# Expert weights, token rows and value tiles asked for in another order in a Trainium2 decoder kernel

## The chip, the core and the metric

One core of a Trainium2 chip runs the whole kernel in one launch. Its engines are PE (matrix products), DVE and POOL (elementwise work), ACT (activation functions and copies out of PSUM) and SP (used here to ask for DMA transfers); they run side by side and wait for each other through semaphores. All transfers between the chip's DRAM and SBUF are DMAs. The metric is the device time of one execution in microseconds (us). All data is fp32.

## What is computed

A decoder of two layers runs on x (4 sequences of 512 tokens, 256 wide) with a context `ctx` (4 x 1601 x 256). Every step is followed by a residual sum and a layernorm:

```python
x = ln(x + ttt(x))               # per token one SGD step on W, b, then W@q + b
x = ln(x + cross(x, ctx))        # one head of 256, a 512x1601 side bias
x = ln(x + experts(x))           # 8 experts, each token goes to 2 of them
x = ln(x + causal_self(x))       # 16 heads of 16
x = ln(x + cross_rope(x, ctx))   # 16 heads of 16, rotary positions, mask
x = ln(x + ffn(x))               # 256 -> 1024 -> 256, dequantized weights, SiLU

def expert(xf, e):
    h = gelu(xf @ Wi[e] + bi[e]) * sigmoid(xf @ Wg[e] + bg[e])   # 256 -> 1024
    r = xf + (h @ Wo[e] + bo[e])                                 # 1024 -> 256
    return (r - mean(r)) * rsqrt(var(r) + eps) * gamma[e] + beta[e]
```

The router takes the softmax of `x @ Wr + br`, keeps the two largest experts of each token and weights their outputs by these two probabilities, scaled to the sum 1.

## The kernel before, in words

**Order.** Nearly all of the program stands in sections of `tc.manual_schedule()`: each engine gets its instructions in the order in which the Python code issues them. Nothing is reordered by a planner around the change, so what stands in front of what on an engine or on a DMA queue is decided by the order of the calls. Tiles come from pools with a fixed number of buffers for each name (`bufs`); a tile that is asked for while all its buffers are taken makes its first writer, often a DMA, wait until the oldest one has been read.

**Stages, in us from the start of the profiled execution.** TTT runs to about 270, the first cross attention to 529, the experts from 529.34 to 1008.62; then attention (causal self attention and cross attention with rope, in units of one sequence and some heads) and the last FFN run to 2423.5.

**End of the first cross attention.** The loop over `steps` (a step is 128 tokens of one sequence) scores, transposes and sums up the weighted context rows. What follows for a sequence, the closing layernorm, the transposes of x, the router and the scatter of its rows into per-expert row lists `xs`, is a generator, `closing(b)`, of which `tail()` runs one more piece. For the last sequence no further steps are there to run beside it. The rope attention's values of contexts 2 and 3 (13 tiles of 128 context rows each, 26 calls of `value(b, k)`) are put there: one 128x256 product into a PSUM tile from `bank()`, and a copy by ACT into a row of 16 heads with a column of ones each. `rows_of_values` prepares those rows by DVE memsets. The tuple `(0, 4, 0, 0, 0, 12, ...)` says how many values follow each piece of the tail; the ten left over come after `blocks_left()`, which computes on the chip which rows and weights the pair blocks below need (`xrow`, `wrow`, and a count). The finished rows go to DRAM as `vd[2]` and `vd[3]`.

**Experts.** A block is 256 token rows. A block of kind "f" (first) is the first 256 rows of an expert: weights and rows come through SP's queue from known places. A block of kind "m" (more) is a pair of 128-row halves, which may belong to two different experts: rows are asked for by POOL with an indirect DMA per half (`rows_of`, index `xrow`), and so are the weights (`load_expert`, index `wrow`), for each half its own `eWi`, `eWg` and `eWo`. An `eWo` tile of 1408 KB also holds the bias, the scale (gamma) and the shift (beta). The order is "ffmfmfmmfmfmmfmfmmm", 19 blocks. For each block `i`, `run` calls

- `first_half`: 2 x 64 products with eWi into gelu and with eWg into sigmoid, the product `g` by DVE; as soon as a weight tile has been read, the next block's is asked for (`eWi`, `eWg` have two buffers in `pmw`);
- `turned` of the next block: four transposes of its rows `xb` by PE, copied to `xbT` by DVE;
- `second_half` of the block before: 2 x 16 products with eWo, the residual sum (L991) and bias by DVE, moments and the square root, the layernorm (L999), then scale and shift and the store to `ys`.

The end of `second_half` is what the change touches. For each half it reads in the kernel before

```python
eng = nc.gpsimd if nxt else nc.vector
eng.tensor_tensor(r[:, hs], r[:, hs], gam, ALU.mult)
eng.tensor_tensor(r[:, hs], r[:, hs], bet, ALU.add)
... # the store of r to ys
for half in range(2) if len(wos) == 1 else (h,):
    if nxt:
        weights_of(nxt, "eWo", half)
```

and after both halves `rows_of(after)`. `nxt` is the block after the one that this second half belongs to, `after` the one two further on. `eWo`, `rb` (the tile of `r`), `g` and `xbT` have two buffers in `p3`, `xb` has three. Between the blocks `next(work)` runs one piece of `attention_first`, small preparations of the attention stage.

**Start of attention.** When the count says that no expert has rows left over, `rest` (a branch) is skipped and attention begins. The two expert outputs of each token are gathered by POOL and summed; x is normalized and transposed. The first keys and values do not depend on x: `keys0` are the rope keys of context 0, two calls of `key` (one for each half of the features) for each of the four chunks of 512, 512, 512 and 65 context rows. `key` makes a product, lets ACT write it with its bias to a `raw` tile (four buffers), calls `rotated` (a DVE shuffle, then two products with the cosine and sine tables and a sum by the engine `eng`, L1281 to L1284) and stores it to `kcd` in DRAM, from where it is read back head by head. `key`'s engine is chosen as `nc.gpsimd if here is None or i % 2 else nc.vector`, inside a lambda that reads `eng` when it runs; the loop's last `i` is 3, so that every key of context 0 runs on POOL. `values_tile` makes the tile of values `v0` with two memsets. The order of the first calls is written out by hand:

```python
for f in keys0[0:2] + values1[:8] + add + values1[8:] + turn + keys0[4:6]:
    f()
for f in (k0_, q0_, rows0, *self_values(0), *keys0[2:4], *keys0[6:8]):
    f()
```

`add` sums the expert outputs into x (L1221), `turn` transposes it, `k0_` and `q0_` are keys and queries of the self attention, `rows0` reads them back in the layout for heads. L1401 is the first DVE operation of the attention units on scores (it adds the causal bias and finds the row maximum).

Of the kernel before, what the change touches and what calls it, by code (L numbers as in the profile page):

```python
# [9 lines left out]
F32 = mybir.dt.float32  # L10
# [3 lines left out]
ALU = mybir.AluOpType  # L14
# [3 lines left out]
P = 128  # L18
# [21 lines left out]
def decoder(ctx: ExitStack, tc: tile.TileContext, a: dict, out: bass.AP):  # L40
# [358 lines left out]
    def load_expert(e, names, pool):  # L399

        ts = []
        for name in names:
            t = pool.tile([P, a[name].shape[1]], F32, tag=name, name=name)
            if isinstance(e, int):
                nc.sync.dma_start(t, a[name][e * P : (e + 1) * P, :])
            else:
                nc.gpsimd.indirect_dma_start(
                    t, None, a[name], bass.IndirectOffsetOnAxis(ap=e, axis=0)
                )
            ts.append(t)  # L410
        return ts
# [214 lines left out]
    with tc.tile_pool(name="p2", bufs=2) as p2, ExitStack() as ordered:  # L626
# [138 lines left out]
        values, places = [], {}  # L765

        def rows_of_values():
            big = p2in.tile([P, NT * S2], F32, tag="fs", name="v23")
            rest = p2in.tile([P, KHALF * D], F32, tag="ctxa", name="v2")
            for i in range(NKT):  # L770
                places[3, i] = big[:, i * VROW : (i + 1) * VROW]
                j = NKT + i
                places[2, i] = (
                    big[:, j * VROW : (j + 1) * VROW] if i < 9 else rest[:, (i - 9) * VROW : (i - 8) * VROW]
                )
            for b_ in (2, 3):
                nc.vector.memset(places[b_, NKT - 1], 0.0)
            for t in (big[:, : 22 * VROW], rest[:, : 4 * VROW]):
                t = t.rearrange("p (k r) -> p k r", r=VROW)
                nc.vector.memset(t[:, :, NH * VW :], 0.0)  # L780
                heads = t[:, :, : NH * VW].rearrange("p k (h r) -> p k h r", r=VW)
                nc.vector.memset(heads[:, :, :, HD : HD + 1], 1.0)

        def value(b, k):
            kn = kn_of(k)
            ps = bank()[:, :D]
            mm(ps[:kn], [(ctxTs[b][:, c, k * P : k * P + kn], xaV[:, c, :]) for c in range(2)])
            dst = places[b, k][:kn, : NH * VW].rearrange("p (h r) -> p h r", r=VW)
            nc.scalar.copy(dst[:, :, :HD], ps[:kn].rearrange("p (h r) -> p h r", r=HD))
            if b == 2 and k == NKT - 1:  # L790
                nc.sync.dma_start(vd[2][:, : 9 * VROW], big_of(2, 0, 9))
                nc.sync.dma_start(vd[2][:, 9 * VROW :], big_of(2, 9, NKT))
            if b == 3 and k == NKT - 1:
                nc.sync.dma_start(vd[3], big_of(3, 0, NKT))
# [9 lines left out]
        for i in range(len(steps) + 1):  # L804
# [8 lines left out]
            if i < len(steps):  # L813
                turned(*steps[i])
            tail()
# [8 lines left out]
        values = [lambda b=b, k=k: value(b, k) for b in (2, 3) for k in range(NKT)]  # L824


        for n in (0, 4, 0, 0, 0, 12, 0, 0, 0, 0, 0):
            if n == 4:
                tail()
                rows_of_values()  # L830
            else:
                tail()
            for f in values[:n]:
                f()
            values = values[n:]
# [44 lines left out]
    def values_tile(pool, name, n):  # L880
        t = pool.tile([P, n, NH * VW + HD - 1], F32, tag=name, name=name)
        nc.gpsimd.memset(t[:, :, NH * VW :], 0.0)
        heads = t[:, :, : NH * VW].rearrange("p k (h r) -> p k h r", r=VW)
        nc.gpsimd.memset(heads[:, :, :, HD : HD + 1], 1.0)
        return t


    with tc.tile_pool(name="p3", bufs=2) as p3, ExitStack() as ordered:
# [87 lines left out]
        def second_half(block, nxt, after):  # L976
# [6 lines left out]
            for h in range(2):  # L983
# [19 lines left out]
                eng = nc.gpsimd if nxt else nc.vector  # L1003
                eng.tensor_tensor(r[:, hs], r[:, hs], gam, ALU.mult)
                eng.tensor_tensor(r[:, hs], r[:, hs], bet, ALU.add)
# [4 lines left out]
                for half in range(2) if len(wos) == 1 else (h,):  # L1010
                    if nxt:
                        weights_of(nxt, "eWo", half)
            if after:
                rows_of(after)

        def attention_first():
# [40 lines left out]
            ready["vals"] = [values_tile(p4a, "v0", NKT)]  # L1057
# [50 lines left out]
        def run(blocks, work):  # L1108
# [4 lines left out]
            for name in ("eWi", "eWg", "eWo"):  # L1113
                for h in range(2):
                    if (blocks[0], name) not in first_loads:
                        weights_of(blocks[0], name, h)
            turned(blocks[0])
            for i, b in enumerate(blocks):
# [3 lines left out]
                if i:  # L1122
                    second_half(blocks[i - 1], b, get(i + 2))
# [3 lines left out]
            second_half(blocks[-1], None, None)  # L1127
# [30 lines left out]
    with ExitStack() as s4:  # L1158
# [17 lines left out]
        def one():  # L1176
            return spare() if alone else ps1.tile([P, 512], F32, tag="one", name="one")

        diagq, later_, qt, kself, ngs, vself, vals = (
            ready[k] for k in ("diagq", "later", "qt", "ks", "ngs", "vself", "vals")  # L1180
        )
        kcross = group_tiles(p4c, "kc", S2)
# [122 lines left out]
        def context(b, keys, values, here=None):  # L1305
# [20 lines left out]
            for i in sorted({*keys, *values}):  # L1326
# [5 lines left out]
                eng = nc.gpsimd if here is None or i % 2 else nc.vector  # L1332
# [406 lines left out]
        for f in (k0_, q0_, rows0, *self_values(0), *keys0[2:4], *keys0[6:8]):  # L1739
            f()  # L1740
# [246 lines left out]
```

## Time and profile before

| | us |
|---|---|
| three executions | 2431.46, 2424.82, 2430.93 |
| their median | 2430.93 |
| the profiled execution, its own time | 2425.35 |
| its span (first to last instruction) | 2423.5 |
| PE busy | 2289.2 (94%) |
| DVE busy | 1197.9 (49%) |
| ACT busy | 1063.4 (44%) |
| POOL busy | 435.3 (18%) |
| expert stage, first eWi to last eWo product | 479.28, PE busy 432.99 |
| attention and FFN, 1104 to the end | 1319.6, PE busy 1300.7 |

The page of the profile first gives busy times, then forty slices of 60.6 us with the busy share of each engine in tenths. PEclk in the slices is the clock that the throttle granted to PE, in tenths of full speed. "L202" is line 202 of the kernel's program; nearly all products go through one helper, so they are told apart by their tiles (`bank<-eWo,g`). In an answer on waits a row reads: the engine and tile that waited, what ended the wait, the sum of us, how many waits, the longest. In a timeline a row reads: start, duration, engine, line, operation, output and inputs, the number of instructions, and in brackets the idle time before it and what ended that.

### The profile page before, as it was taken

The page shows a single profiled execution, that of the slowest core. Times are in us where ns is not written, and L with a number is a line of the kernel's source. Part 1 is how long each engine was busy: PE and PEld are TensorE (multiplying, and loading weights), DVE is VectorE, ACT ScalarE, POOL GpSimd, SP SyncE. Part 2 cuts the span into 40 slices and gives each one's busy share as a digit, 9 for nine tenths or more (in the row PEclk, how much of TensorE's full clock was granted, in tenths as well). Part 3 has the DMA queues.
Part 4 walks back from the last instruction along what each step waited for, and adds up shares of the span by engine and source line. Part 5 has one row for each costly group of instructions (what it writes and reads, how often), then busy time and mean ns, then how long its engine had stood idle before and what let it go on. Part 6 is the DMA issues. An engine that isn't in the chain of part 4 may idle for free.

```text
span 2423.5 us, 36202 instructions
## 1 busy us (share of the span) xinstructions
PE 2289.2 (94%) x14448; PEld 1296.1 (53%) x14448; DVE 1197.9 (49%) x2846; ACT 1063.4 (44%) x2103; POOL 435.3 (18%) x455
## 2 busy tenths in 40 slices
PE   7898999979898999789999999999999999999998
PEld 4767677768787888643333334333333333333266
DVE  2343334422232332226666667666766776677334
ACT  1211222124445454234555553655665666556730
POOL 1010001121333334274330010120122010000000
PEclk9999999989999999888999998999999999999999
DMA  8300211145788767432210220111120010100100
GB/s 328 145 1 22 110 55 45 52 165 207 288 327 313 276 264 291 145 115 70 79 44 27 72 72 1 32 38 46 52 73 28 25 59 15 58 6 18 31 9 27
DMA packets 77099, 244.13 MB, mean 101 GB/s; under 512 B 11640, under 2 KB 34686, under 8 KB 64638
## 3 DMA queue, kind: packets, MB, share of 16 engines
q1 hardware_dynamic: 60126, 137.41, 16.7%
q0 software_dynamic: 13632, 89.32, 9.7%
q10 hardware_dynamic: 3168, 15.03, 1.7%
q8 instruction: 116, 1.90, 0.3%
q14 instruction: 57, 0.47, 0.1%
HBM read 196.12 MB, written 56.77 MB: 104 GB/s over the span
## 4 chain that ended last, share of the span: by engine, by line
PE 50%; DVE 1%; ACT 1%; issue 0%; DVEq 0%; ACTq 0%
PE s L1442 23%; PE po L1469 12%; PE one L202 11%; PE s L202 2%; PE s L1452 1%; PE one L1427 1%; PE one L1490 1%; ACT x L171 0%; ACT ex L1456 0%; DVE pm L1399 0%; DVE one L1401 0%; PE one L1511 0%; PE one L1609 0%; PE one L1532 0%; DVE nb L166 0%
## 5 line engine op out<-in xcount | busy, mean ns | idle before, releaser
L1456 ACT ACTIVATE ex<-s 128x512 f32<-128x512 f32 (+1 forms) x1062 | 578.2, 594 | 460.7 <-PE s L1442 225.6
L1399 DVE TENSOR_REDUCE pm<-one 128x1 f32<-128x512 f32 x768 | 493.1, 685 | 162.7 <-PE s L1442 106.9
L1442 PE MATMUL s<-q,kc 32*128 32x512 f32 x1612 | 529.9, 640 | 0.9 <-ACT ex L1456 0.8
L202 PE MATMUL one<-kc,qt 32*128 32x512 f32 (+1 forms) x2048 | 484.4, 564 | 0.3 <-DVE pm L1399 0.3
L1442 PEld LDWEIGHTS s<-q,kc 32*128 32x128 f32 x1612 | 166.3, 179 | 204.1 <-issue 170.4
L1469 PE MATMUL po<-ex,v 128*32 128x256 f32 (+3 forms) x2688 | 252.2, 444 | 0.3 <-ACT ot L1482 0.3
L1401 DVE CUSTOM_DVE_ANT_0 one<-one,c_diagq 128x512 f32<-128x512 f32 x256 | 171.9, 716 | 74.3 <-PE one L202 62.3
L1469 PEld LDWEIGHTS po<-ex,v 128*32 128x32 f32 (+1 forms) x2688 | 54.2, 108 | 253.1 <-issue 246.4
L1442 PE MATMUL s<-q,ks 32*128 32x512 f32 x512 | 180.0, 651 | 5.4 <-ACT ex L1456 4.9
L202 PEld LDWEIGHTS one<-kc,qt 32*128 32x128 f32 x2048 | 164.6, 189 | 11.8 <-DVE pm L1399 7.5
L202 PE MATMUL bank<-eWo,g 128*128 128x256 f32 x608 | 151.9, 410 | 17.1 <-DMA eWo<-in_eWo,wrow 11.3
L202 PE MATMUL one<-ks,qt 32*128 32x512 f32 x512 | 152.6, 665 | 2.2 <-ACT raw L1314 2.2
L1282 POOL TENSOR_TENSOR raw<-raw,c_cos 128x512 f32<-128x512 f32 (+1 forms) x32 | 35.0, 1094 | 629.9 <-DVE swp L1281 570.5
L202 PEld LDWEIGHTS bank<-eWo,g 128*128 128x128 f32 x608 | 123.7, 208 | 40.4 <-issue 10.7
L971 DVE TENSOR_TENSOR g<-g,sg 128x1024 f32<-128x1024 f32 x38 | 46.5, 1224 | 196.4 <-ACT sg L969 177.1
L202 PE MATMUL wide<-xbT,eWi 128*128 128x128 f32 (+1 forms) x960 | 139.5, 306 | 4.0 <-DVE xbT L937 4.0
L202 PEld LDWEIGHTS wide<-xbT,eWi 128*128 128x128 f32 x960 | 130.5, 193 | 12.3 <-issue 3.4
L202 PE MATMUL wide<-xbT,eWg 128*128 128x128 f32 (+1 forms) x960 | 137.0, 303 | 0.0
L202 PEld LDWEIGHTS wide<-xbT,eWg 128*128 128x128 f32 x960 | 128.1, 191 | 6.6
L1442 PEld LDWEIGHTS s<-q,ks 32*128 32x128 f32 x512 | 53.9, 185 | 83.5 <-issue 62.3
L98 ACT ACTIVATE sd<-mv,eps 128x1 f32<-128x1 f32 (+2 forms) x34 | 10.0, 295 | 188.9 <-DVE mv L109 188.8
L202 PE MATMUL wide<-ctxT,q 128*128 128x512 f32 (+1 forms) x256 | 91.3, 510 | 0.8 <-DVE q L667 0.8
(325 smaller groups left out, 3038.2 us busy)
## 6 DMA issues: line engine op xcount, KB each, us to landing
xs<-zero SPq DMA_DIRECT2D x32, 512.0 KB
kc<-kcd SPq DMA_DIRECT2D x16, 800.5 KB
eWo<-in_eWo SPq DMA_DIRECT2D x8, 1408.0 KB
eWi<-in_eWi SPq DMA_DIRECT2D x8, 1028.0 KB
eWg<-in_eWg SPq DMA_DIRECT2D x8, 1028.0 KB
qt<-qd SPq DMA_DIRECT2D x32, 256.0 KB
ctxT<-in_ctxT SPq DMA_DIRECT2D x4, 1601.0 KB
kcd<-in_c_rowkc ACTq DMA_DIRECT2D x4, 1601.0 KB
```

The costliest lines, as they stand in the source:

```text
L98: nc.scalar.activation(sd, mv[:, :, 1], AF.Sqrt, bias=eps)
L202: nc.tensor.matmul(ps, l, r, start=(i == 0), stop=(i == n - 1))
L971: nc.vector.tensor_tensor(part, part, dst, ALU.mult)
L1282: eng.tensor_tensor(raw[:, :n], raw[:, :n], cos[:, :n], ALU.mult)
L1399: nc.vector.tensor_reduce(pm[:, t, j, c : c + 1], ps, AX.X, ALU.max)
L1401: nc.vector.tensor_tensor_reduce(out=ps, in0=ps, in1=diagq[:, 384 - t * P : 896 - t * P], scale=1.0, scalar=LOWEST, op0=ALU.add, op1=ALU.m ...
L1427: nc.tensor.transpose(pt[:, t * P : (t + 1) * P], ng.rearrange("p j r -> p (j r)"), ident)
L1442: nc.tensor.matmul(ps[:kn], kt[rows, k * P : k * P + kn], q2[rows, :], start=True, stop=cross)
L1452: nc.tensor.matmul(ps[:, k * P : (k + 1) * P], later_[:, :P], later_[:, P:], start=False, stop=True)
L1456: nc.scalar.activation(ex[:kn, h, :], ps[:kn], AF.Exp)
L1469: nc.tensor.matmul(state["po"][j * 32 : j * 32 + 32, q0:q1], (vals if cross else vself)[b % 2][:kn, k, c0 : c0 + 32], ex[:kn, j % 2, q0:q1 ...
L1490: nc.tensor.transpose(pt[:, t * P : (t + 1) * P], ot[:, t * P : (t + 1) * P], ident)
```

## The change

It has four parts.

1. In the expert stage `eWo` gets three buffers in place of two. `second_half` asks for the rows of the block two further on first, and for output weights after that, through a new helper `outs`, which keeps a list of all halves of all blocks in order and asks for the next ones whenever fewer than three are taken.
2. Scale and shift of each expert output go to DVE, for all blocks; before, this was so for the last block alone.
3. At the end of the first cross attention the values of contexts 2 and 3 are computed in another order, two to a double PSUM tile from `wide()`, and spread differently over the pieces of the tail; the rows that hold them are prepared in two parts, the large one inside the loop over `steps`.
4. At the start of attention all rotations of context 0's keys go to DVE, the self values come after the keys, and `v0` has a pool of its own on the other side of SBUF, with its memsets on DVE.

The core of the diff (the lines before and after are in the functions printed above; "..." stands for lines left out):

```diff
@@ load_expert
-            t = pool.tile([P, a[name].shape[1]], F32, tag=name, name=name)
+            t = pool.tile(
+                [P, a[name].shape[1]], F32, tag=name, name=name, bufs=3 if name == "eWo" else 2
+            )
@@ end of the first cross attention
-        def rows_of_values():
...
+        def rows_of_values(first):
+
+            name, tag, n = ("v23", "fs", 22) if first else ("v2", "ctxa", 4)
+            t = p2in.tile([P, NT * S2 if first else KHALF * D], F32, tag=tag, name=name)
+            for i in range(n):
+                at = (3, i) if first and i < NKT else (2, i - NKT) if first else (2, 9 + i)
+                places[at] = t[:, i * VROW : (i + 1) * VROW]
+            nc.vector.memset(places[3 if first else 2, NKT - 1], 0.0)
...
         def value(b, k):
             kn = kn_of(k)
-            ps = bank()[:, :D]
+            if not halves or len(halves) == 2:
+                halves[:] = [wide()]
+            else:
+                halves.append(halves[0])
+            ps = halves[0][:, len(halves) - 1, :D]
...
-            if b == 2 and k == NKT - 1:
+            if (b, k) == (2, 8):
                 nc.sync.dma_start(vd[2][:, : 9 * VROW], big_of(2, 0, 9))
+            if (b, k) == (3, NKT - 1):
+                nc.sync.dma_start(vd[3], big_of(3, 0, NKT))
+            if (b, k) == (2, NKT - 1):
                 nc.sync.dma_start(vd[2][:, 9 * VROW :], big_of(2, 9, NKT))
-            if b == 3 and k == NKT - 1:
-                nc.sync.dma_start(vd[3], big_of(3, 0, NKT))
...
             if i < len(steps):
                 turned(*steps[i])
+            else:
+                rows_of_values(True)
...
-        values = [lambda b=b, k=k: value(b, k) for b in (2, 3) for k in range(NKT)]
-
-
-        for n in (0, 4, 0, 0, 0, 12, 0, 0, 0, 0, 0):
-            if n == 4:
+        order = [(2, k) for k in range(9)] + [(3, k) for k in range(NKT)]
+        order += [(2, k) for k in range(9, NKT)]
+        values = [lambda b=b, k=k: value(b, k) for b, k in order]
+        for n in (3, 0, 0, 0, 0, 0, 6, 0, 0, 0, 0, 0):
+            if len(values) < len(order):
                 tail()
-                rows_of_values()
-            else:
-                tail()
+            if len(values) == len(order) - 3 and len(places) == 22:
+                rows_of_values(False)
@@ second_half
-        def second_half(block, nxt, after):
+        def second_half(block, after, outs):
...
-                eng = nc.gpsimd if nxt else nc.vector
-                eng.tensor_tensor(r[:, hs], r[:, hs], gam, ALU.mult)
-                eng.tensor_tensor(r[:, hs], r[:, hs], bet, ALU.add)
+                nc.vector.tensor_tensor(r[:, hs], r[:, hs], gam, ALU.mult)
+                nc.vector.tensor_tensor(r[:, hs], r[:, hs], bet, ALU.add)
...
-                for half in range(2) if len(wos) == 1 else (h,):
-                    if nxt:
-                        weights_of(nxt, "eWo", half)
             if after:
                 rows_of(after)
+            outs(len(wos))
@@ run
-            for name in ("eWi", "eWg", "eWo"):
+            for name in ("eWi", "eWg"):
...
+            ahead = [(b, h) for b in blocks for h in range(len(halves(*b)))]
+            taken = [0]
+
+            def outs(free):
+                taken[0] -= free
+                while ahead and taken[0] < 3:
+                    b, h = ahead.pop(0)
+                    weights_of(b, "eWo", h)
+                    taken[0] += 1
+
+            outs(0)
...
-                    second_half(blocks[i - 1], b, get(i + 2))
+                    second_half(blocks[i - 1], get(i + 2), outs)
@@ attention
-            ready["vals"] = [values_tile(p4a, "v0", NKT)]
+        pv0 = s4.enter_context(tc.tile_pool(name="pv0", bufs=1, side="right"))
+        vals = [values_tile(pv0, "v0", NKT, nc.vector)]
...
-                eng = nc.gpsimd if here is None or i % 2 else nc.vector
+                eng = nc.gpsimd if here is None else nc.vector
...
-        for f in (k0_, q0_, rows0, *self_values(0), *keys0[2:4], *keys0[6:8]):
+        for f in (k0_, q0_, rows0, *keys0[2:4], *keys0[6:8], *self_values(0)):
             f()
```

More of the change, by code (lines that the diff above doesn't have):

```diff
@@ L764, in decoder @@
         xaV = weight(p2, "xaV")
-        values, places = [], {}
-        def rows_of_values():
[L768 to L782, printed above, removed]
+        values, places, halves = [], {}, []
+        def rows_of_values(first):
[5 more added lines that the diff above has]
+            nc.vector.memset(places[3 if first else 2, NKT - 1], 0.0)
+            t = t[:, : n * VROW].rearrange("p (k r) -> p k r", r=VROW)
+            nc.vector.memset(t[:, :, NH * VW :], 0.0)
+            heads = t[:, :, : NH * VW].rearrange("p k (h r) -> p k h r", r=VW)
+            nc.vector.memset(heads[:, :, :, HD : HD + 1], 1.0)
         def value(b, k):
             kn = kn_of(k)
-            ps = bank()[:, :D]
+            if not halves or len(halves) == 2:
[3 more added lines that the diff above has]
+            ps = halves[0][:, len(halves) - 1, :D]
             mm(ps[:kn], [(ctxTs[b][:, c, k * P : k * P + kn], xaV[:, c, :]) for c in range(2)])
@@ L878, in group_tiles, with values_tile @@
         ]
-    def values_tile(pool, name, n):
+    def values_tile(pool, name, n, eng=nc.gpsimd):
         t = pool.tile([P, n, NH * VW + HD - 1], F32, tag=name, name=name)
-        nc.gpsimd.memset(t[:, :, NH * VW :], 0.0)
+        eng.memset(t[:, :, NH * VW :], 0.0)
         heads = t[:, :, : NH * VW].rearrange("p k (h r) -> p k h r", r=VW)
-        nc.gpsimd.memset(heads[:, :, :, HD : HD + 1], 1.0)
+        eng.memset(heads[:, :, :, HD : HD + 1], 1.0)
         return t
@@ L1126, in run @@
                 next(work, None)
-            second_half(blocks[-1], None, None)
+            second_half(blocks[-1], None, outs)
         order = "ffmfmfmmfmfmmfmfmm" + "m" * 1
@@ L1177, in one @@
             return spare() if alone else ps1.tile([P, 512], F32, tag="one", name="one")
-        diagq, later_, qt, kself, ngs, vself, vals = (
-            ready[k] for k in ("diagq", "later", "qt", "ks", "ngs", "vself", "vals")
-        )
+        diagq, later_, qt, kself, ngs, vself = (
+            ready[k] for k in ("diagq", "later", "qt", "ks", "ngs", "vself")
+        )
+        pv0 = s4.enter_context(tc.tile_pool(name="pv0", bufs=1, side="right"))
+        vals = [values_tile(pv0, "v0", NKT, nc.vector)]
         kcross = group_tiles(p4c, "kc", S2)
```

## The prediction

> **What bounds the kernel now.** I read the page's forty slices first, then PE's waits by stage, then the timelines around the waits.
>
> ```profile
> PE   7898999979898999789999999999999999999998
> ...
> PEclk9999999989999999888999998999999999999999
> DMA  8300211145788767432210220111120010100100
> ```
>
> A slice is 60.6 us. From slice 19 on PE is at 9 or 10 tenths: attention binds on PE and the change leaves it alone. What can move are the holes of slices 8, 12 and 16 to 18, and the dips of PEclk beside them. The waits of PE from 529 to 1009 us, the expert stage:
>
> ```profile
> PE bank L933 <- DMA xb<-xs,xrow: 24.0, 7, 5.8
> PE bank L202 <- DMA eWo<-in_eWo,wrow: 11.3, 4, 6.9
> PE bank L933 <- DMA xb<-xs: 7.9, 2, 6.6
> PE bank L202 <- DVE rb L991: 5.2, 9, 0.6
> ```
>
> The first three rows, token rows (`xb`) and output weights (`eWo`) that come late, are what the change aims at. Of the 7.9 us, 6.6 end at 529.34, where the stage begins. One such hole:
>
> ```profile
> 770.93 1.27 POOL L1004 TENSOR_TENSOR rb<-rb,eWo 128x512 f32<-128x512 f32 x1 [21.34 <-DVE rb L999]
> ...
> 773.70 0.98 POOL L407 DMA_INDIRECT eWo<-in_eWo,wrow  x1 [0.15 <-issue]
> ...
> 776.25 0.96 POOL L922 DMA_INDIRECT xb<-xs,xrow  x1 [0.31 <-issue]
> ...
> 786.52 1.16 PE L933 MATMUL bank<-ident,xb 128*128 128x128 f32 x4 [5.67 <-DMA xb<-xs,xrow]
> ...
> 787.47 5.88 PE L202 MATMUL bank<-eWo,g 128*128 128x256 f32 x16
> ...
> 793.93 3.72 PE L202 MATMUL bank<-eWo,g 128*128 128x256 f32 x16 [0.57 <-DVE rb L991]
> ```
>
> POOL scales and shifts `rb`, asks for two eWo halves (2 x 1408 KB), and only then for xb; PE wanted xb at 780.85. After the hole the 16 matmuls take 5.88 us, later 3.72. The start of attention has the next hole:
>
> ```profile
> 1053.79 1.27 POOL L1282 TENSOR_TENSOR raw<-raw,xT 128x512 f32<-128x512 f32 x1
> ...
> 1061.90 0.60 ACT L1256 ACTIVATE raw<-one 128x512 f32<-128x512 f32 x1 [10.57 <-DMA kcd<-raw]
> ...
> 1062.56 2.07 PE L202 MATMUL one<-qkvV,xT 128*128 128x256 f32 x4 [6.79 <-ACT raw L1256]
> ...
> 1081.40 0.69 DVE L1401 CUSTOM_DVE_ANT_0 one<-one,c_diagq 128x512 f32<-128x512 f32 x1
> ```
>
> POOL rotates the first keys only at 1053.79 (until then it sums expert outputs), `raw` tiles stay taken, ACT and PE stop, and DVE's first L1401 waits until the last rotation.
>
> **What the Trainium skill says.** Three places. "TensorE: Matmul & The Clock Gate", Part 1: after about 3.4 us of idling the array's clock is halved until it has been busy as long again. The trace agrees: after holes of 3.6 to 5.8 us four transposes take 0.8 to 1.16 us, otherwise 0.60. "GPSIMD Engine Reference", 3.1: a two-input fp32 elementwise operation is about twice as slow on GpSimd as on the vector engine; here 128x512 takes 1267 ns on POOL and 692 on DVE (L995). "DMA: Bandwidth & Descriptors", "Issuing engines are not separate DMA queues": all transfers share 16 engines, whoever asks. The trace fits: with DMA share 1.00 it moves 415 to 425 GB/s.
>
> **The change part by part.**
>
> 1. *Expert stage, xb and eWo.* Idle that goes: 24.0 + 11.3 + 1.3 (the 7.9 less 6.6) = 36.6 us. xb is now asked for once the previous block's rb addition (L991) has read its tile, before eWo: in the case shown near 768 in place of 776.25, ahead of 2.9 MB instead of behind. (A single block's xb goes by SP, behind the previous ys store as before, but now ahead of eWo.) Those 2.9 MB are 6.9 us at 415 GB/s, so xb is there by about 771, 10 us before its use. eWo runs one half ahead by a third tile; the halves that made PE wait at 712, 718 and 835 are asked for before the intervening first half (14 us or more of PE) instead of after. Only the last half still follows closely: asked near 990 (its tile is free when DVE ends the scaling of block m9's first half, L999 at 988.8 plus 2 x 0.43), 7.0 us to land as at 990.64 to 997.65, so 997; PE would want it at 990.4 + 3.7 = 994.1: 2.8 us stay.
>
>  Clock that comes back: batches of 16 matmuls after holes took 6.10, 4.81, 5.88, 5.38, 5.31, 5.81 and 6.66 us against 3.69, an excess of 14.1; transposes 1.14, 1.13, 0.77, 1.16, 0.81, 1.14 against 0.60, 2.6. Sum 36.6 + 16.7 - 2.8 = 50.5. I take 3 off for stray DMA waits: **-47**, bounds -33 (4 us at most of three or four holes return) and -52.
>
> 2. *Scale and shift on DVE.* 19 blocks: 8 x 2 x 0.69 + 22 x 2 x 0.43 = 30 us of DVE work, of which the last block's was there already. DVE is busy 134 of 479 us in this stage; behind the added 0.9 to 1.4 us stand L991 of the second half, `g` and xbT, each with over 5 us until PE needs it, and ACT's sqrt of the second half, with gelu behind it, whose PSUM tile PE wants 13 us after the stage's eWi begins. Zero on the path; if that cover were gone, 22 x 0.9 = 19 us. POOL loses 49 us of work and with it the delay of its requests (counted in 1). The ys stores on SP now wait for DVE alone, about 1 us sooner.
>
> 3. *End of the first cross attention.* Before, the DVE memsets (486.24 to 488.2) hold PE for 4.68 us with two single banks of values; now the large tile is prepared earlier (1.3 us of DVE, beside PE's 10 us of weighted sums) and three double banks take three values without a stop. Transposes of x come at 486.4 instead of 491.9. PE's twelve values before routing's matmul (13.65 us from 499.18, while DVE waits 7.54) become six. Routing ends near 501 instead of 514.4, the scatter near 512. But 17 values follow instead of 10: 17 x 0.86 = 14.6, the last near 515. And SP's queue, as the built program has it, puts both xb and both eWo of the first experts behind eight attention weights and four small rows, and these wait for the landing of all three `vd` stores: vd3 asked for at 512, 2.5 MB at 372 GB/s (530 to 540) plus 2 us: 520.7. From there the eight weights take 5 us and four rows 0.75 each (as from 534.78 to 543.55), xb is asked for at 528.7 and lands 3 us later: 531.7, against 529.34. So the earlier routing is given back: **+2**, bounds -4 and +8. Where the stall goes: from scatter to that queue.
>
> 4. *Start of attention.* All eight rotations of context 0 move to DVE: 0.63 + 3 x 0.65 = 2.6 us for a wide key (DVE starts 128x512 operations 0.65 apart, as L1401 at 1082.01 and 1082.65) instead of 3.8 on POOL. Keys 0 and 1 now stand ahead of the sums of x (L1221): these move from 1035.6 to 1039.5, and the transposes of x, which wait for them, from 1046.1 to 1049. Then, in before's clock: k0 and q0 reach `raw` at 1055.1 and 1056.8 (its tiles are long free), qd is read back at 1062.2 (4.75 us, as 1066.38 to 1071.13), key 4's store is asked for at 1063.6 and lands 4.6 us later (as 1072.51 to 1077.12), the narrow keys follow, and the first scores begin near 1070.7, the second group at 1077.2 where it was 1084.68: -7.5. Self values moved behind the keys fill the wait. I take **-8**, bounds 0 (the store's wait grows) and -13. Two memsets of v0 move from POOL to DVE, 0.7 us at 1016, before ACT's first copy at 1018.37: zero, at most +0.7. From 1104 on nothing is changed, and PE, busy 1300.7 of 1319.6 us, carries a shift to the end.
>
> Sum: -47 + 2 - 8 = -53. The profiled execution took 2425.35 us (span 2423.5 and 1.85 around it): 2372.3. The three runs have their median at 2430.93, 5.6 above; less 53 it is 2378. I take **2374**.
>
> **The rivals.**
>
> A. *DMA takes half back* (0.17): asking for eWo a half earlier puts 1408 KB ahead of eWi and eWg, and in the three runs of adjacent pair blocks these come late. For: DMA share is 0.90 to 1.00 from 730 to 740 and around every hole. Against: the stage averages 273 GB/s, and PE has no wait for eWi or eWg today. Price: 11 pair blocks x 2 us = 22: 2396.
>
> B. *The stage begins much later* (0.08): the queue of part 3 costs 15 us more, because weights and stores slow each other: 2387.
>
> C. *Slower* (0.03): eWi behind two eWo halves in every pair block, 2.9 MB = 6.9 us, plus 1.5 us of cold clock, 11 times: +92, less 53 from 2427, between the two bases: 2466. It decides once the free time of DMA before eWi's use falls under 5 us per block; the window 760 to 770 with share 0.34 speaks against it.
>
> D. *The holes close but the end does not move* (0.02), if attention had slack against its own DMA: 2425. PE's 98.6% there excludes most of it.
>
> **How the numbers follow.** The forecast has 0.70 with its own range 2362 to 2388 (parts 1, 3 and 4 seldom err the same way). With A and B inside, 2360 to 2398 leaves out 2 in 10. A measurement of this kernel tells 0.3% (7 us) from no change: faster 0.95, same 0.02, slower 0.03.
>
> **What would show it.** Right: no row "DMA xb<-xs,xrow" among PE's waits and under 4 us for eWo; the stage from first eWi to last eWo near 432 us instead of 479; the first xb landing near 531 with PE idle some 15 us before it; L1401 some 10 us sooner after the stage's start. Wrong: a new wait of PE for eWi or eWg; PE waiting for a DVE result in the expert stage over 6 us; PE idle before the first block over 22 us.

## The result, and the profile after

| | before | after |
|---|---|---|
| seven executions, median, us | 2426.52 | 2403.76 |
| lowest and highest | 2422.43, 2434.26 | 2400.13, 2416.31 |
| profiled execution, its span | 2423.5 | 2400.8 |

The ratio is 0.9908, with a 95% interval of 0.9884 to 0.9931: about 22 us less, clear of the measurement's uncertainty. The forecast was 53 us less, so the direction is right, the size less than half.

I cut both spans at the same marks: the first transposes of expert rows, the end of the last eWo product, the first product of attention behind the branch.

| stage, us | before | after | moved | forecast |
|---|---|---|---|---|
| start to the first transposes of `xb` | 529.34 | 546.81 | +17.5 | +2.4 |
| expert stage | 479.28 | 446.95 | -32.3 | -47 |
| end of it to the first product of attention | 7.62 | 7.62 | 0 | 0 |
| attention and FFN to the end | 1407.3 | 1399.4 | -7.8 | -8 |

The sum is -22.7. In the page's forty slices of the changed kernel, counted from 0, the holes in slices 8 (6 tenths) and 16 to 17 remain, while slice 12 has closed:

```profile
PE   7899999968999999889999999999999999999998
...
PEclk9999999988999999989999998999999999999999
DMA  8400311135887867341210210111110010100000
```

**The late start.** The timeline of the changed kernel around the end of the first cross attention (start, duration, engine, line, operation):

```profile
507.89 0.34 SPq L793 DMA_DIRECT2D vd<-v  x1
...
515.28 2.00 PE L202 MATMUL wide<-xaV,ctxT 128*128 128x256 f32 x8 [0.46 <-ACT v L791]
...
517.74 1.99 PE L202 MATMUL wide<-xaV,ctxT 128*128 128x256 f32 x8 [0.46 <-ACT v L791]
...
524.17 0.34 SPq L795 DMA_DIRECT2D vd<-v  x1
...
529.03 0.32 SPq L797 DMA_DIRECT2D vd<-v  x1
531.87 0.38 SPq L79 DMA_DIRECT2D qkvQ<-in_qkvQ  x1
...
542.73 0.25 SPq L85 DMA_DIRECT2D xa_bo<-in_xa_bo  x1
543.54 1.07 SPq L922 DMA_DIRECT2D xb<-xs  x2
...
546.81 1.08 PE L939 MATMUL bank<-ident,xb 128*128 128x128 f32 x4 [18.22 <-DMA xb<-xs]
```

Two values now take 2.45 us: their products run for 1.99 us, then PE waits 0.46 us for ACT's second copy. The last `vd` store is asked for at 529.03, the first attention weight follows 2.8 us later (POOL's next request, too, waited for that store to land), the twelve requests last until 543.54, and only then comes `xb`. PE is idle for 18.22 us.

**The expert stage.** PE's waits in it, from 546.81 to 993.76 (what waited, what ended the wait, sum of us, number, longest):

```profile
PE bank L939 <- DMA xb<-xs: 24.6, 5, 18.2
PE bank L202 <- DVE rb L997: 10.7, 11, 3.2
PE wide L202 <- DVE xbT L943: 4.0, 2, 3.2
PE bank L202 <- DMA eWo<-in_eWo,wrow: 2.9, 1, 2.9
```

The row for rows that POOL asks for (`xb<-xs,xrow`, 24.0 us before) is gone, and eWo fell from 11.3 to 2.9 us. But the rows of single blocks, which SP asks for, now cost 24.6 - 18.2 = 6.4 us where they cost 1.3, and the wait for DVE's `rb` doubled from 5.2 to 10.7. Idle time in the stage is 24.0 us, was 46.3; PE's busy time is 422.97, was 432.99.

One late row tile, in the timeline of the changed kernel:

```profile
751.89 0.56 ACTq L879 DMA_DIRECT2D kcd<-in_c_rowkc  x1
...
754.26 0.37 SPq L922 DMA_DIRECT2D xb<-xs  x1
754.51 0.94 POOL L409 DMA_INDIRECT eWo<-in_eWo,wrow  x1 [3.30 <-DMA ys<-rb]
...
768.01 0.63 PE L939 MATMUL bank<-ident,xb 128*128 128x128 f32 x4 [3.46 <-DMA xb<-xs]
```

These 256 KB of rows take 13.7 us. In the window 744 to 768 the DMA share is 1.01 at 421 GB/s, and the queues of POOL (q0), SP (q1) and ACT (q10) divide it so (packets, MB, share):

```profile
q0 software_dynamic: 788, 6.47, 64.3%
q1 hardware_dynamic: 736, 1.98, 20.7%
q10 hardware_dynamic: 48, 1.64, 15.9%
```

The Trainium skill, "DMA: Bandwidth & Descriptors", section "Queues, rings and completion order", says that each DMA engine goes round the queues that have work, packet by packet. The counts agree with that but do not prove it: SP's 736 packets are nearly as many as POOL's 788, but a packet of SP's carries 2.7 KB on average and one of POOL's 8.2. In this window SP's queue had a fifth of the bandwidth, and the rows shared it with stores and an `eWi` of the same queue.

The gathered weights are not the only candidate. Each of the four late row tiles (asked for at 599.36, 642.21, 710.07 and 754.26) follows within some 3 us on loads for attention that ACT asked for, 1.0 to 1.6 MB each time, like the `kcd` of 1.6 MB above. The two single blocks later in the stage (824.78 and 871.56) have no such load beside them, and their rows are not late. Before the change the same loads ran too and SP's rows cost 1.3 us in all, so the loads alone do not explain it; no run takes them away, and the shares of the two stay open.

One of the two long waits for `rb`:

```profile
846.05 1.64 SPq L1068 DMA_DIRECT2D mi<-in_mask  x4
...
858.00 0.52 DVE L1072 TENSOR_SCALAR mf<-mi 16x401 f32<-16x401 int32 x1 [12.86 <-DMA mi<-in_mask]
...
859.04 2.34 DVE L977 TENSOR_TENSOR g<-g,sg 128x1024 f32<-128x1024 f32 x2
861.31 0.67 DVE L943 COPY xbT<-bank 128x512 f32<-128x512 f32 x1
861.91 0.40 DVE L997 TENSOR_TENSOR rb<-bank,xb 128x256 f32<-128x256 f32 x1
```

A piece of the attention mask, four requests of 6.3 KB each, lands 10 us after the last of them was asked for, and DVE's queue stands still behind the step that reads it. The gate product `g`, `xbT` and `rb` are then done one after another, PE waits 3.02 us for `rb`, and the 16 products after it take 5.17 us instead of 3.72.

### The profile page after: what moved, and what is told of

Same layout as the page of the kernel before. It is cut to its first block, busy times and chain, and to the rows that moved or that the text cites. A ratio compares the mean times of both kernels' runs of the same rounds, so it can differ in the third digit from the quotient of the medians.

```text
span 2400.8 us, 36163 instructions
## 1 busy us (share of the span) xinstructions
PE 2275.6 (95%) x14448; PEld 1289.9 (54%) x14448; DVE 1239.0 (52%) x2928; ACT 1064.2 (44%) x2103; POOL 360.0 (15%) x373
## 3 DMA queue, kind: packets, MB, share of 16 engines
q1 hardware_dynamic: 60126, 137.41, 16.7%
## 4 chain that ended last, share of the span: by engine, by line
PE 50%; DVE 1%; ACT 1%; issue 0%; DVEq 0%; ACTq 0%
PE s L1458 23%; PE po L1485 12%; PE one L202 11%; PE s L202 2%; PE s L1468 1%; PE one L1443 1%; PE one L1506 1%; ACT x L171 0%; ACT ex L1472 0%; DVE pm L1415 0%; DVE one L1417 0%; PE one L1527 0%; PE one L1625 0%; PE one L1548 0%; DVE nb L166 0%
## 5 line engine op out<-in xcount | busy, mean ns | idle before, releaser
L1417 DVE CUSTOM_DVE_ANT_0 one<-one,c_diagq 128x512 f32<-128x512 f32 x256 | 171.8, 716 | 76.0 <-PE one L202 65.1
L202 PE MATMUL bank<-eWo,g 128*128 128x256 f32 x608 | 141.9, 390 | 13.6 <-DVE rb L997 10.7
L977 DVE TENSOR_TENSOR g<-g,sg 128x1024 f32<-128x1024 f32 x38 | 46.3, 1223 | 178.5 <-ACT sg L975 178.5
L202 PEld LDWEIGHTS bank<-eWo,g 128*128 128x128 f32 x608 | 116.4, 196 | 33.5 <-DVE rb L997 14.8
L975 ACT ACTIVATE g<-wide,eWi 128x128 f32<-128x128 f32 (+1 forms) x240 | 72.6, 415 | 27.0 <-PE wide L202 26.8
```

The costliest lines, as they stand in the source:

```text
L202: nc.tensor.matmul(ps, l, r, start=(i == 0), stop=(i == n - 1))
L975: nc.scalar.activation(dst[:, k, :], pv[:, k, :], func, bias=bias)
L977: nc.vector.tensor_tensor(part, part, dst, ALU.mult)
L1417: nc.vector.tensor_tensor_reduce(out=ps, in0=ps, in1=diagq[:, 384 - t * P : 896 - t * P], scale=1.0, scalar=LOWEST, op0=ALU.add, op1=ALU.m ...
```

## The experiments

Most parts of the late start, the stage and attention were tried apart; that rows are asked for ahead of eWo was not tried alone. For the start I count from the end of the last weighted sums of the first cross attention to the first transposes of `xb`. The profiled executions reach that end between 481.9 and 487.6 us (482.14 before, 487.26 after), which is decided in the first 180 us, in code that no kernel here touches. For the start of attention I count from its first product to the eighth diagonal-bias step of DVE (L1401 before, L1417 after). Ratios are to the kernel before, run beside each kernel, with their 95% intervals; the changed kernel was not run again beside the experiments.

| kernel | sums to rows | expert stage | eighth step | ratio |
|---|---|---|---|---|
| before | 47.2 | 479.3 | 71.9 | 1 |
| after | 59.6 | 447.0 | 67.5 | 0.9908 (0.9884 to 0.9931) |
| e1_rows_first | 50.2 | 449.7 | 65.3 | 0.9848 (0.9828 to 0.9868) |
| e2_rows_first_old_values | 52.4 | 443.6 | 67.5 | 0.9854 (0.9835 to 0.9873) |
| e3_v0_pool_only | 61.9 | 483.8 | 72.8 | 1.0050 (1.0033 to 1.0068) |
| e4_rotations_only | 45.8 | 484.5 | 67.8 | 0.9980 (0.9953 to 1.0007) |
| e5_mask_early | 63.4 | 442.3 | 67.4 | 0.9844 (0.9816 to 0.9872) |
| e6_rows_one_block_earlier | 60.7 | 438.2 | 68.1 | 0.9857 (0.9827 to 0.9886) |
| e7_two_ahead | 57.0 | 448.5 | 70.2 | 0.9897 (0.9863 to 0.9931) |
| e8_scale_on_pool | 62.0 | 458.0 | 67.5 | 0.9932 (0.9906 to 0.9958) |
| e9_rows_first_single_values | 40.2 | 445.6 | 65.1 | 0.9810 (0.9780 to 0.9839) |
| e10_keys_before_turn | 62.9 | 449.8 | 64.8 | 0.9867 (0.9837 to 0.9897) |
| e11_all | 40.2 | 429.0 | 62.0 | 0.9710 (0.9682 to 0.9738) |

Each stage is from one profiled execution. How far such a number wanders is seen where kernels share the code of a stretch. In the first column six kernels have the changed kernel's code up to the rows (after, e5 to e8, e10) and lie between 57.0 and 63.4 us. In the second, five have its expert stage (after, e1, e2, e9, e10) and lie between 443.6 and 449.8; the three with the stage before (before, e3, e4) between 479.3 and 484.5. In the third, nine have its order of work at the start of attention (after, e1, e2, e4 to e9) and lie between 65.1 and 70.2. Differences inside these ranges decide nothing.

**e1_rows_first**, on the changed kernel (`late` holds the twelve requests for attention weights and small rows):

```diff
-            W[name] = weight(plw, name)
+            W[name] = plw.tile([P, 2, a[name].shape[1]], F32, tag=name, name=name)
...
             outs(0)
+            while late:
+                late.pop(0)()
             turned(blocks[0])
```

> The changed kernel, but SP asks for the rows and output weights of the first blocks before the eight attention weights and four small rows (12 requests), which follow in the same queue. Nothing else is moved. Theory Q (the 18.2 us hole ahead of the experts is the place in SP's queue): xb is asked for at 529.4, right behind the third vd store, and lands 3.1 us later as in the kernel before, so the first transposes stand near 532.5 instead of 546.8, and the cold clock behind the long hole (about 3 us in the first two blocks) comes back: 14 to 18 us less than the changed kernel, 2386 to 2390. Rival D (the DMA engines are full with vd stores and scatter, and the rows would land late from any place in the queue): transposes at 543 or later, gain under 4 us, 2400 or more.

The timeline of PE in this kernel:

```profile
536.86 1.09 PE L945 MATMUL bank<-ident,xb 128*128 128x128 f32 x4 [6.18 <-DMA xb<-xs]
```

The hole is 6.2 us instead of 18.2. `xb` was asked for at 533.97, once the third store (531.11) had landed. From sums to rows it is 9.4 us less, from the last value to the rows 12.0. Theory Q holds: the place in the queue is most of the hole. The whole gain is a little less than expected, 2392.55 in the median against 2428.66 before.

**e3_v0_pool_only**, on the kernel before: `v0` leaves `p4a` for the pool `pv0`, as in the diff of the change, and its memsets go to DVE.

> The kernel before, with v0 in a pool of its own and its memsets on DVE, and nothing else of the change. In the built program this alone puts the eight attention weights and four small rows ahead of the first xb in SP's queue. Theory Q: the weights wait for the vd3 store (asked for at 526.6, landed near 532.4), take 5.9 us, the small rows 5.7, xb is asked for near 544 and lands near 547: expert stage 17 to 18 us later than before, 2443 to 2448 with the colder clock behind the hole. Rival D: no change beyond 4 us, 2423 to 2431.

The requests in the kernel before, then in this kernel:

```profile
526.20 0.37 SPq L916 DMA_DIRECT2D xb<-xs  x1
526.63 0.46 SPq L794 DMA_DIRECT2D vd<-v  x1
```

```profile
530.46 0.32 SPq L794 DMA_DIRECT2D vd<-v  x1
536.36 0.38 SPq L79 DMA_DIRECT2D qkvQ<-in_qkvQ  x1
...
547.63 1.09 PE L933 MATMUL bank<-ident,xb 128*128 128x128 f32 x4 [21.03 <-DMA xb<-xs]
```

`xb` is asked for at 544.19; the rows come 14.7 us later behind the sums than before (61.9 against 47.2), and the kernel is 0.5% slower. So the move of one tile to another pool (with its two memsets), which looks like bookkeeping, is what put the weights in front of the rows. The loads of the attention weights stand between two sections of written order, so the description of the kernel before, by which nothing around the change is reordered, does not hold for them: they are placed by the scheduler, and it placed them elsewhere once the pools had changed. Why the tile was moved is argued, not shown: the third eWo tile takes 11 KB of each of the 128 partitions (1408 KB in all), and that room had to come from somewhere.

The weights are not the whole delay. Before, the first `xb` was asked for ahead of the third `vd` store; here the first weight follows 5.9 us behind that store, and the twelve requests take 7.8 us more. In e1_rows_first `xb` stands ahead of the weights but still behind the store, and follows the last request of the scatter that writes the rows by 14.6 us (519.39 to 533.97), where it was 2.5 us before the change (523.73 to 526.20). This goes with the hole of 6.2 us that is left there. No run puts the rows ahead of the store again.

**e2_rows_first_old_values** (part 3 taken out of e1_rows_first) and **e9_rows_first_single_values** (part 3's order kept in it, but each value in a bank of its own):

```diff
-            if not halves or len(halves) == 2:
-                halves[:] = [wide()]
-            else:
-                halves.append(halves[0])
-            ps = halves[0][:, len(halves) - 1, :D]
+            ps = bank()[:, :D]
```

> e1_rows_first with part 3 undone: value tiles in single banks and in the order of the kernel before, all row memsets at once. Theory V (part 3 costs, because pairs of value tiles take 2.45 us and the last vd store is asked for at 529.0 instead of 526.6): first transposes near 530, 2 to 3 us sooner than in e1_rows_first, and the whole 2 to 3 us faster than it. Rival: part 3 pays, as the memset hole of 4.68 us comes back: stage begins 2 us or more later than in e1_rows_first.

> e1_rows_first with part 3's order of values kept, but each value in a single bank instead of two to a double one. Theory P (in pairs PE waits 0.46 us for ACT's second copy at each pair, 2.45 us a pair, where single banks ran 0.92 us a value): the 17 late values take 16 instead of 21 us, the third vd store is asked for some 5 us sooner, the rows wait for it to land as in e1_rows_first, and the first transposes come 3 to 5 us sooner than there (536.86). Rival D (the large vd store in front holds the DMA engines, whenever PE is ready): under 2 us sooner.

The timeline of PE in e9_rows_first_single_values:

```profile
504.97 15.25 PE L202 MATMUL bank<-xaV,ctxT 128*128 128x256 f32 x68
...
527.82 1.09 PE L941 MATMUL bank<-ident,xb 128*128 128x128 f32 x4 [7.59 <-DMA xb<-xs]
```

All 17 late values follow each other without a stop: 15.25 us, 20.7 in the changed kernel. From sums to rows: 52.4 with the old order, 50.2 with the new order in pairs, 40.2 with the new order in single banks. In pairs the new order is worth nothing that can be told (2.2 us), in single banks 12; I had expected that single banks bring 3 to 5 us, and they bring 10. Theory P holds and was too small: the 17 late values gain 6.4 us against e1_rows_first, and 5.0 us come from the values ahead of them; the landing of the last store takes 1.4 us of it back. Theory V had a saving of 2 to 3 us for the old order, which does not show.

**e4_rotations_only**, the kernel before with `eng = nc.gpsimd if here is None else nc.vector` and the self values behind the keys; **e10_keys_before_turn**, the changed kernel with

```diff
-        for f in keys0[0:2] + values1[:8] + add + values1[8:] + turn + keys0[4:6]:
+        for f in keys0[0:2] + values1[:8] + add + values1[8:] + keys0[2:4] + turn + keys0[4:6]:
...
-        for f in (k0_, q0_, rows0, *keys0[2:4], *keys0[6:8], *self_values(0)):
+        for f in (k0_, q0_, rows0, *keys0[6:8], *self_values(0)):
```

> The kernel before with only the rotations of context 0's keys on DVE and the self values behind the keys. Theory (prediction, step 4): from the start of attention to the end 8 us less (1407.3 to 1399.4 us), expert stage as before: 2418. Rival: the 7.8 us seen between the two kernels came from v0's memsets or from DMA traffic left over from the expert stage; then under 3 us.

> The changed kernel with the second chunk's two wide keys of context 0 moved ahead of the transposes of x, so that no wide key waits for a raw tile after the self keys and queries. Theory R (the first scores stand 60.5 us behind the start of attention because the four raw tiles are held until the ksd and qd stores have landed, and two wide keys and two narrow ones queue for them): first L1417 (L1401 before the change) 4 to 7 us sooner after the start of attention than the 62.4 us of the changed kernel. Rival: the transposes of x come as much later (they wait for ACT and DVE, which the keys keep busy), under 2 us.

With the rotations and the later self values alone the eighth step comes 4.2 us sooner (71.9 to 67.8), in the whole change 4.4, and v0's pool alone gives nothing (72.8): these two are the gain, but half of the 8 us. The ratio of e4 by itself does not tell it from no change. The timeline of the changed kernel shows what is late instead (1001.38 is the stage's first product):

```profile
1044.19 0.58 SPq L1202 DMA_DIRECT2D ksd<-raw  x1
...
1048.35 0.69 ACT L1330 ACTIVATE raw<-one,bk 128x512 f32<-128x512 f32 x1 [2.47 <-DMA ksd<-raw]
...
1057.83 0.32 ACT L1330 ACTIVATE raw<-one,bk 128x65 f32<-128x65 f32 x1 [5.91 <-DMA kcd<-raw]
...
1061.91 2.06 PE L202 MATMUL one<-ks,qt 32*128 32x512 f32 x8
```

Four `raw` tiles hold two keys, the self keys and the self queries; the next keys wait until the store of the self keys has landed, and the narrow ones until theirs have. In e10_keys_before_turn ACT's waits for the stores of `raw` fall from 11.9 to 5.9 us, and the first step stands 57.8 us behind the stage's first product; in the changed kernel it is 62.4, in the other eight kernels with its order there 59.8 to 64.0. So theory R holds for the waits and the first step, with 2 us or more. At the eighth step the gain does not show: 64.8 is hardly below the 65.1 and 65.3 that e9 and e1 have without this edit. More tiles for `raw` were not tried.

**e5_mask_early**, the changed kernel with two `mi` tiles, each piece of the mask asked for one block ahead of its use:

```diff
+                nxt = mask_of(k0 + 401) if c < 3 else None
                 nc.vector.tensor_scalar(mf, mi, 0.0, MASKED, ALU.is_equal, ALU.mult)
...
+                mi = nxt
                 yield
```

> The changed kernel, in which each piece of the mask is asked for one block ahead of the DVE step that reads it (two mi tiles in place of one); the steps of the mask end one block later. Theory M (the two 3 us waits of PE for DVE's rb at 862 and 910 come from DVE standing in front of a mask piece that lands 10 to 12 us after its request): both waits fall to 0.6 us, the two batches of products behind them from 5.2 to 3.7 us, and the expert stage from 446.95 to about 439. Rival S (it is the scale and shift that DVE now does): waits and stage as in the changed kernel, 446 to 448.

PE's waits in its expert stage:

```profile
PE bank L939 <- DMA xb<-xs: 26.6, 5, 17.9
PE bank L202 <- DVE rb L997: 5.4, 10, 0.6
```

The two long waits are gone and the rest is the 0.5 to 0.6 us of before: theory M. DVE's added 30 us of scale and shift are not in it. The stage is 4.6 us shorter than in the changed kernel, 3 fewer than expected, as the rows of single blocks cost 26.6 - 17.9 = 8.7 us here. With 442.3 us it is only just below the range of the five kernels above, so the waits are the proof, not the stage.

**e6_rows_one_block_earlier** (`xb` with `bufs=4`, `rows_of(get(i + 3))`) and **e7_two_ahead** (`taken[0] < 2` in place of 3), both on the changed kernel:

> The changed kernel with four xb tiles and every block's rows asked for one block earlier. Theory X (PE's 6.4 us of waits for xb<-xs inside the expert stage are rows that SP asks for in good order, but that take up to 13.7 us beside output weights): these waits fall under 1 us and the stage from 446.95 to about 440. Rival A (the DMA engines are full, so that what is moved ahead makes something else late): the sum of PE's waits for xb and eWo stays near 9 us, stage 445 or more.

> The changed kernel with its three eWo tiles, but only two halves taken ahead, so that a pair block's weights are asked for after the second half of the block before has freed them, as before the change, though still behind the rows. Theory (the third tile is worth the eWo waits and costs the SP rows their speed): waits for eWo rise from 2.9 to about 8 us with some 4 us of cold clock, waits for xb<-xs inside the stage fall from 6.4 to 2 or less; stage 449 to 454. Rival (order alone is worth the gain, and the third tile is idle): stage within 2 us of 446.95.

PE's waits in the expert stage of e6_rows_one_block_earlier, then of e7_two_ahead:

```profile
PE bank L939 <- DMA xb<-xs: 18.3, 1, 18.3
PE bank L202 <- DVE rb L997: 11.0, 11, 3.3
...
PE bank L202 <- DMA eWo<-in_eWo,wrow: 2.6, 1, 2.6
```

```profile
PE bank L939 <- DMA xb<-xs: 14.6, 1, 14.6
PE bank L202 <- DMA eWo<-in_eWo: 10.6, 4, 5.2
PE bank L202 <- DVE rb L997: 7.7, 11, 2.5
```

In both no row is late inside the stage (the one wait left is the start). Asking a block earlier removes it at no price in time (it takes a fourth `xb` tile), 8.7 us off the stage. Holding back the third eWo tile moves the wait to the eWo that SP asks for, 10.6 us in four waits, and the stage is 1.6 us longer, which is less than such a stage wanders. With rows asked for so late the third tile therefore brings nothing that can be told; what it brings with rows asked for earlier was not tried.

**e8_scale_on_pool**, the changed kernel with

```diff
-                nc.vector.tensor_tensor(r[:, hs], r[:, hs], gam, ALU.mult)
-                nc.vector.tensor_tensor(r[:, hs], r[:, hs], bet, ALU.add)
+                eng = nc.vector if block == ("more", 10) else nc.gpsimd
+                eng.tensor_tensor(r[:, hs], r[:, hs], gam, ALU.mult)
+                eng.tensor_tensor(r[:, hs], r[:, hs], bet, ALU.add)
```

> The changed kernel with scale and shift back on POOL for all blocks but the last, nothing else moved. Theory (prediction, step 2: zero on the path): expert stage within 3 us of 446.95; the 49 us of work on POOL delay some requests by 1 to 3 us. Rival S (DVE's added 30 us hold rb, which PE waits for): PE's waits for rb fall from 10.7 to about 5 us, stage 440 to 442. Rival P (POOL's work ahead of its requests was part of what made rows and weights late): stage 453 or more.

PE's waits in its expert stage:

```profile
PE bank L939 <- DMA xb<-xs: 26.8, 4, 19.5
PE bank L202 <- DVE rb L997: 9.5, 11, 3.2
PE bank L202 <- DMA eWo<-in_eWo,wrow: 7.0, 1, 7.0
...
PE bank L939 <- DMA xb<-xs,xrow: 2.7, 4, 1.2
```

Rival P: the stage is 11.0 us longer. POOL's rows come late again in four places, and the last eWo waits for POOL to read its tile, then lands 7.0 us late as before the change. `rb` hardly moves, so rival S is wrong.

**e11_all** puts e9, e5, e6 and e10 together.

> The changed kernel with all that helped or is expected to: rows asked for before the attention weights, single banks for values, mask pieces one block early, four xb tiles with rows one block earlier, the second chunk's keys ahead of the transposes. Theory (the gains add, as they are at different places in time): 12 + 4 + 5 + 9 + 5 = 35 us less than the changed kernel, 2365 to 2373. Rival (what is asked for earlier crowds the DMA engines at the start of the experts): 2380 or more.

PE's waits in its expert stage:

```profile
PE bank L941 <- DMA xb<-xs: 7.6, 1, 7.6
PE bank L202 <- DVE rb L999: 5.5, 10, 0.6
PE wide L202 <- DVE xbT L945: 4.0, 2, 3.2
PE bank L202 <- DMA eWo<-in_eWo,wrow: 3.4, 1, 3.4
```

2361.75 us in the median, 2430.98 for the kernel before beside it: ratio 0.9710 (0.9682 to 0.9738), better than both kernels and 3 us below the range that was expected. The stage of 429.0 us is below the 432 that the prediction gave for the change, and the rows come 40.2 us behind the sums. The gains add, as was argued from their different places in time. The hole of 7.6 us before the first rows is left: here, too, `xb` is asked for behind the third `vd` store.

## Why the prediction was wrong, step by step

**Step 3, the end of the first cross attention: +2 forecast, +17.5 measured.** The order in the queue was seen and the reason too; the sizes failed, one after another. Values were taken at 0.86 us each, from the kernel before, though they had moved to pairs: with waits for ACT they ran 1.23. The six values ahead of routing's matmul kept PE until 507.3, so that routing was late as well. The last store was asked for at 529.0, not near 515, and the first weight at 531.9, not 520.7: 11.2 us late. The eight weights took 6.0 us, not 5, the four rows 5.7, not 3.0, the landing 3.3: another 4. Of the 11.2 us, 5.1 were there before any changed line ran (the sums ended at 487.26 instead of 482.14); the other 6.1 are in the main the pacing of the values (17 took 20.7 us, 14.6 were reckoned). Counted from the end of the sums the change costs 12.4 us. The size is that of rival B, "the stage begins much later", which had 15 us more and a chance of 0.08, but this is luck: its reason, weights and stores that slow each other, is at most the 4 us.

**Step 1, xb and eWo: -47 forecast, -32.3 measured.** What the step said of POOL's rows held to the tenth (24.0 us gone), as did the last eWo (2.8 forecast, 2.9 measured). Two terms failed. The 1.3 us of SP's rows were to go because these are asked for ahead of eWo; being ahead in one queue was no help against another queue, and they became 6.4. This is rival A at another tile: eWi and eWg are never late, the rows are. The same loads of ACT stand beside the late rows, so how much is POOL's weights and how much is theirs stays open. And the wait for `rb` was carried over at 5.2 us. DVE had waited for the mask pieces before the change as well (36.1 us in four waits, 40.0 after), but beside PE's holes; with PE early, PE waits behind them, +5.5. Together they make 11.9 us; other waits changed by half a microsecond, and the idle time is 11.5 above the forecast. The clock gave back 10.0 us of PE's busy time, not 16.7, and most of the difference is in four batches that ran slow: 5.17 and 5.23 us behind `rb` and 5.20 behind the last eWo, all three against 3.7, and 10.02 instead of 7.14 us for the second block's eWi. This last one stands behind a wait of 3.2 us for `xbT` in both kernels and was slow in one alone, so why is open. 11.5 + 6.7 less the 3 taken off for stray waits is 15.2; the stage missed by 14.7.

**Step 2, scale and shift on DVE: zero.** Right for DVE (e5_mask_early leaves nothing of `rb` to explain). That POOL is relieved was counted in step 1, and e8_scale_on_pool prices it: 11 us. Without it part of POOL's rows would still be late.

**Step 4, the start of attention: -8 forecast, -4.4 measured.** The -7.8 between the two profiled executions agrees by accident. The failed term is "k0 and q0 reach `raw` ... its tiles are long free": that is so for those two, but not for the two wide keys behind them, which wait 2.5 and 2.2 us for the stores of the self keys and queries; the step followed the narrow keys alone. The remaining 3.4 us lie behind the eighth step, in code that is the same in all thirteen kernels and took 1325.6 to 1335.5 us in their profiled executions (1335.4 before, 1332.0 after). They fit a stretch of slower PE in the execution of the kernel before:

```profile
2168.60 0.69 PE L1442 MATMUL s<-q,kc 32*128 32x512 f32 x1
...
2171.99 1.22 PE L1442 MATMUL s<-q,kc 32*128 32x512 f32 x1
...
2178.49 0.69 PE L1442 MATMUL s<-q,kc 32*128 32x512 f32 x1
```

From 2171.0 to 2177.9 the granted clock was 0.51, and each product takes nearly twice its time. The changed kernel has no such stretch there; e1_rows_first has one.

So the range (2360 to 2398) missed because two steps failed the same way at once, of which I had said that they seldom do. They have one thing in common: each took the time of a value, a transfer or a wait from the kernel before, and the change had altered its form or what ran beside it. One of the signs named for being wrong came true: PE waits for a DVE result in the expert stage, `rb`, for 10.7 us, over the 6 us that were set. Two slips in the sums decide nothing: 22 x 0.9 is 19.8, not 19, and rivals A and B start from 2374 and from 2372. Rival C (weights late in every pair block) and rival D (no change) found nothing: PE has no wait for eWi or eWg.

## What to carry to other kernels

When requests are reordered, list for every queue what stands in front of the moved one, and for every transfer what the other queues move in the same microseconds: here small rows beside large loads had to be asked for a whole block ahead. A move of a tile between pools can change the order of DMA requests that nobody wrote down, so read the built order around every pool that changes, and write the order of those that matter. When PE becomes early, look for the steps that were late but hidden behind its old holes; the next wait is among them.

## What had not been expected of the hardware

- PE slows to about half for some 7 us in the middle of dense work: in the kernel before at 2171 us the same product takes 1.22 instead of 0.69 us at a granted clock of 0.51, and PE was busy for 20.80 of the 21 us in front of it, with no idle time over 0.20 us. The Trainium skill, "TensorE: Matmul & The Clock Gate", Part 1, ties the half clock to idling, in a whole window or in frequent short gaps; nothing like that precedes it here, and the measurement decides. It costs 3 to 4 us, an estimate from half of its length. It is not scattered: six of the thirteen profiled executions (before, e1, e5, e9, e10, e11) have it at the same place, 1081 to 1083 us behind the eighth step (in e10 for half as long), and seven do not. Its cause was not looked for.
- A transfer of 256 KB took 13.7 us while all DMA engines together moved 421 GB/s, and a piece of the mask, four times 6.3 KB, took 10 us at another place.
